# Beginning of the attention: whose engine makes the token sums, in which stages the first pair's queries and keys are made, and who orders TensorE

## The chip, the cores and the metric

The kernel runs on one core of a Trainium2 chip, as one launch. The metric is the device time in microseconds (us); lower is better. A core has a matrix engine (TensorE, PE in the profile; its weight loads are PEld), a vector engine (VectorE, DVE), a scalar engine (ScalarE, ACT), a general engine (GpSimd, POOL) and a queue that issues transfers (SyncE, SP). Each works through its own queue in order and waits for the others by semaphores.

## The reference

A block of three layers on x of 4 sequences by 256 tokens by 512 features, all in 32-bit floats:

```python
x = x + 0.5 * ffn(layernorm(x), A, B, Wr)      # 64 experts of rank 16, top 16 by softmax gates
x = x + attn(layernorm(x), wq, wkv, wo)
x = x + 0.5 * ffn(layernorm(x), A, B, Wr)

def attn(h, wq, wkv, wo):                      # 32 heads of 128
    q = (h @ wq) per head, first 128 of 192 columns
    k, v = (h @ wkv) per head
    scores = q @ k.T * 192 ** -0.5, causal
    return (softmax(scores) @ v) @ wo
```

The part that the change touches is the passage from the first feed-forward layer to the attention: the layer norm of the last tokens, and the queries, keys and values of the first heads.

## The kernel before

**Products in seven instead of eight.** Each large product is cut into 2x2 blocks, and sums of blocks let seven block products stand for eight. A product has a left side (tokens) and a right side (weights), and each needs its sums. `left_sums` (L166 to L175) makes the four sums of a left side, `right_sums` (L177) those of a right side. `seven` (L189) yields after each of the seven products M1, M2, M6, M5, M7, M3, M4; they use three PSUM banks: M1, M6, M7 and M4 one after the other in the first, M2 in the second, M5 and M3 in the third. After a product a reader takes the bank's sum out (L160, L139): ACT copies or VectorE adds. The next product into that bank waits for the reader.

Queries, keys and values use this scheme **twice**, one level inside the other. The tokens are held in `xop` as 7 outer by 7 inner operands, each 128x256. An outer index stands for one of the outer seven products (M1 0, M2 1, M7 2, M4 3, M5 4, M6 5, M3 6); the inner sums of one outer operand are the four sums of its own blocks (`inner_sums`, L450: inner 4, 5 and 6, and inner 2 overwritten in place). One **stage** makes one or two outer products with all their inner seven, and its readers add them to where they belong. So the values of a block of heads take stages for M1, M2, M6, M4 with M7, M5 and M3.

The weights are loaded block by block by SP and their sums made on GpSimd (`two_levels`, L505): first M5 and M6 (L525, L526), then the inner sums (L181, L184 to L186). M7 and M4 overwrite M1 and M2 in place once these have been used: `t3` (L518) and `t4` (L521), each 128x896.

**Loops.** Heads come in 16 pairs. `make_qk` (L594) makes queries and keys of a pair while the pair before attends, and `make_v` (L768) the values of two pairs at a time. The stages of pair 1 and later are M1 with M5, M2 with M6, M7 with M3, and M4. For the first pair they are M1, M2, M6 with M5, M7 with M3, and M4, in another set of readers. `qk` of a pair has four blocks of results; block 2 of the first pair is set to zero by a memset on GpSimd (L664), since M5's reader adds to it. In the stages that have an `into`, GpSimd adds two blocks of the result after the last read of each part (`done`, L650). Values have a form with M4 and M7 of their own (`m47`, L745): ACT copies one half of the bank, VectorE adds the other, and GpSimd sums the halves afterwards (L753).

**The beginning of the attention.** `norm_pair` (L457) is what the first layer calls after each pair of token tiles: normalise, transpose on TensorE, copy (L470 and L479 to L482) and form outer sums (L472 to L477). After the last tiles VectorE also forms outer 6's inner 2 and 3 (L484, L485). Then L896 to L915 interleave the first values' and the first pair's products, seven steps each at a time, with the last norm between the first and second seven, and inner sums between the third ones:

```python
    take(first_layer, 1)
    for _ in range(7):
        take(first_v, 1)
        take(first_qk, 1)
    inner_sums(5, 6, nc.vector)
    inner_sums(4, 5, nc.vector)
    inner_sums(2, 3, nc.gpsimd)
    inner_sums(6, 7, nc.gpsimd)
```

and `inner_sums(3, 4, nc.vector)` after the third seven. What is left of these streams goes into the eight units of pair 0's attention, by the letters in `FIRST_UNITS` (L942): g is the first values, f the first pair's queries and keys, v and q the next ones, b the second half of an attention block (`attend`, L867, after `probs`, L828).

**What sets the order.** A scheduling layer puts the instructions of each engine into an order of its own, by its estimate, unless an instruction is held with `keep_in_program_order`. Before, only the statistics of the norms (L103) and the first sum of the first output weights (L183) are held.

Of the kernel before, what the change touches and what calls it, by code (L numbers as in the profile page):

```python
# [32 lines left out]
def macaron_kernel(  # L33
# [11 lines left out]
    nc = tc.nc  # L45
# [117 lines left out]

    LAST = (3, 4, 5, 6)

    def left_sums(eng, s, a11, a12, a21, a22, *of):  # L166


        s3 = s[3] if len(s) > 3 else a21
        r11, r12, r21, r22 = of or (a11, a12, a21, a22)  # L170
        eng.tensor_tensor(s[0], r21, r22, ALU.add)  # L171
        eng.tensor_tensor(s[1], s[0], r11, ALU.subtract)
        eng.tensor_tensor(s[2], r12, s[1], ALU.subtract)
        eng.tensor_tensor(s3, r11, r21, ALU.subtract)
# [64 lines left out]
    def ffn(name, pairs, a_sums, b_sums, after, late):  # L239

        with ExitStack() as scope:
# [165 lines left out]
            for u in range(n + 1):  # L407
                hid = hidden(pairs[u], lefts[u], hgs) if u < n else iter(())
                tokens = prepare(pairs[u + 1]) if u + 1 < n else iter(())
                behind = after(work, pairs[u - 2]) if u > 1 else iter(())  # L410
                take(hid, 1)
                take(behind, 1)
                take(tokens, 1)
                take(hid, 2)
                take(tokens, 1)
                take(hid, 1)
                take(tokens, 1)
                if u < n:
# [12 lines left out]
        yield from after(None, pairs[n - 1])  # L431


# [13 lines left out]

    early = xop[:, 5:7, 6]

    def inner_sums(lo, hi, eng):  # L450
        o = slice(lo, hi)
        blocks = [xop[:, o, i] for i in range(4)]
        if lo == 0:
            blocks[2] = early
        left_sums(eng, [xop[:, o, i] for i in (4, 5, 6, 2)], *blocks)

    def norm_pair(work, pair):  # L457

        half, a = divmod(pair[0] // 2, 2)
        sl = slice(2 * a, 2 * a + 2)  # L460

        where = [xop[:, k, 4:6, :].rearrange("p a s -> p (a s)") for k in (5, 6)]
        tokens = normed(work, pair, "a", where)
        yield
        for i, xn in enumerate(tokens):
            cols = slice(i * P, (i + 1) * P)
            pt = turned_x(xn, f"a_{pair[i]}").rearrange("p (o c) k -> p o c k", o=2)
            a11, a12, s3, a22, s1, s2, _ = (xop[:, k, sl, cols] for k in range(7))
            if half:
                nc.scalar.copy(a22, pt[:, 1])  # L470
                if a:
                    nc.vector.tensor_tensor(s3[:, 0], early[:, 0, cols], pt[:, 0, 0], ALU.subtract)  # L472
                    nc.vector.tensor_tensor(s3[:, 1], a11[:, 1], pt[:, 0, 1], ALU.subtract)
                else:
                    nc.vector.tensor_tensor(s3, a11, pt[:, 0], ALU.subtract)
                nc.vector.tensor_tensor(s2, pt[:, 1], s3, ALU.subtract)
                nc.vector.tensor_tensor(s1, a22, pt[:, 0], ALU.add)  # L477
            elif a:
                nc.scalar.copy(early[:, :, cols], pt[:, :, 0])  # L479
                nc.scalar.copy(xop[:, 0:2, 3, cols], pt[:, :, 1])  # L480
            else:
                nc.scalar.copy(xop[:, 0:2, sl, cols], pt)  # L482
        if half and a:
            nc.vector.tensor_tensor(xop[:, 6, 2], early[:, 1], xop[:, 5, 2], ALU.subtract)  # L484
            nc.vector.tensor_tensor(xop[:, 6, 3], xop[:, 1, 3], xop[:, 5, 3], ALU.subtract)  # L485
        elif half:
            nc.vector.tensor_tensor(xop[:, 6, sl], xop[:, 1, sl], xop[:, 5, sl], ALU.subtract)
        elif a:
            inner_sums(0, 2, nc.vector)

    raw, rights, outs = {}, {}, {}

    def load_o(p):

# [10 lines left out]
    def two_levels(pool, bufs, name, blocks):  # L505

        t = {
            m: pool.tile([P, 7, P], F32, tag="w", name=f"{name}_{m}", bufs=bufs)  # L510
            for m in ("M1", "M5", "M2", "M3", "M6")
        }
        for m, k, n in (("M1", 0, 0), ("M5", 0, 1), ("M2", 1, 0), ("M3", 1, 1)):
            for i, view in enumerate(blocks(k, n)):
                nc.sync.dma_start(t[m][:, i : i + 3 : 2], view)

        def t3():
            nc.gpsimd.tensor_tensor(t["M1"], t["M6"], t["M1"], ALU.subtract)  # L518

        def t4():  # L520
            nc.gpsimd.tensor_tensor(t["M2"], t["M2"], t["M6"], ALU.subtract)  # L521

        def sums():
            plain = {m: v[:, 0:4] for m, v in t.items()}
            nc.gpsimd.tensor_tensor(plain["M5"], plain["M5"], plain["M1"], ALU.subtract)  # L525
# [12 lines left out]
    def load_qk(p):  # L538

        if p < NG:  # L540
            rights["qk", p] = two_levels(
                qkpool,
                6,
                f"wqk_{p}",
                lambda k, n: [
                    view[:, 2 * k : 2 * k + 2, p * HG + n, 0:DN] for view in (wq_v, wk_v)
                ],
            )()

    def load_v(k):  # L550

        if 2 * k < NG:
            raw["v", k] = two_levels(
                vpool,
                5,
                f"wv_{k}",
                lambda c, n: [
                    wv_v[:, 2 * c : 2 * c + 2, (2 * k + n) * HG + j] for j in range(HG)
                ],
            )  # L560

    with ExitStack() as scope:
# [31 lines left out]
    def make_qk(p):  # L594
# [33 lines left out]

            return read

        def branch(blocks, into=None):


            def read(r, ps):
                to = part(blocks, r)
                of = to if READS[r][2] else part(slice(1, 2), r).to_broadcast(to.shape)
                nc.vector.tensor_tensor(to, of, ps, ALU.add)  # L637
                done(r, into)

# [2 lines left out]
        def onto(blocks, into=None):  # L642
            def read(r, ps):
                to = part(blocks, r)
                nc.vector.tensor_tensor(to, to, ps, ALU.add)  # L645
                done(r, into)

            return read

        def done(r, into):  # L650

# [5 lines left out]
        if p > 0:  # L657
# [14 lines left out]
        yield from stage(("M4",), onto(slice(1, 2)), "d")  # L672
# [12 lines left out]
    def v_stages(k):  # L685
# [2 lines left out]
            return {}  # L688
        right, t3, t4 = raw["v", k]()
        u = 2 + 2 * (k % 2)  # L690

        def stage(ms, read, name, behind=None):
            def product(n, ps, first):
# [206 lines left out]
    for _ in range(7):  # L900
        take(first_v, 1)
        take(first_qk, 1)
    take(first_layer, 1)
    for _ in range(7):
        take(first_v, 1)
        take(first_qk, 1)
    inner_sums(5, 6, nc.vector)
    inner_sums(4, 5, nc.vector)
    inner_sums(2, 3, nc.gpsimd)
    inner_sums(6, 7, nc.gpsimd)  # L910
    for _ in range(7):
        take(first_v, 1)
        take(first_qk, 1)
    inner_sums(3, 4, nc.vector)
    take(first_qk, 7)  # L915

# [22 lines left out]
            "qoqobqoqo",  # L939
        ),  # L940
    )
    FIRST_UNITS = ("gfgfbgf", "gfgfbgfgf", "gvqvqbvqvq", "vqvqbvqvqvq", "vqvqbvqvqvq", "vqvqbvqq", "vqvqbqvqq", "vqvqbvqqq")  # L942
    LAST_UNITS = ("", "b", "oob", "oob", "oob", "oob", "ooob", "ooob")
    attending = []
    nothing = iter(())
    for p in range(NG):
# [92 lines left out]
```

## Time and profile before

| | us |
|---|---|
| median of 3 runs | 1184.9 (1184.69 to 1185.73) |
| the profiled execution | 1187.66 |
| its span | 1185.5 |
| chain that ended last: TensorE | 95% of the span |
| VectorE in it | 2% |
| transfers in it | 1% |
| VectorE sum of 128x512 (L824), mean | 0.688 |
| GpSimd sum of 128x256 (L654), mean | 0.728 |

The profile is of one execution, taken by the hardware profiler; its span is the stretch from the first to the last instruction. "Busy" counts the time in which an engine has an instruction in it, and an idle gap is put down to what released it, for example `<-DVE vbuf L721`. Columns of a timeline are start, length, engine, line, operation, output and inputs, partitions by elements, and how many like it follow each other. A 128x256 product is two records on TensorE. In the windows the clock is TensorE's granted one as a share of the full one.

### The profile page before, as it was taken

How to read it: one execution, taken by the hardware profiler on the slowest of the kernel's cores; microseconds unless marked ns; L12 is line 12 of the kernel's file. 1: busy time of each engine (PE TensorE's matmuls, PEld its weight loads, DVE VectorE, ACT ScalarE, POOL GpSimd, SP SyncE). 2: the span in 40 equal slices, each digit the busy share in tenths (PEclk: the TensorE clock that was granted, in tenths of full speed). 3: DMA queues.
4: the chain of work that ended last, by engine and by line, in shares of the span. 5: the costliest groups of instructions: out<-in, count | busy, mean ns of one | idle time of the engine just before them, and what ended most of it. 6: DMA issues, size and time to landing. Idle time of an engine off the chain costs nothing.

```text
span 1185.5 us, 18545 instructions
## 1 busy us (share of the span) xinstructions
PE 1166.3 (98%) x6492; PEld 1005.8 (85%) x6492; DVE 741.7 (63%) x1932; ACT 492.7 (42%) x1364; POOL 676.3 (57%) x933
## 2 busy tenths in 40 slices
PE   8999979999999999999999999999999999999998
PEld 5677869999999999999999898989898988875767
DVE  5444786566666666666576657665766666675432
ACT  4443314534443444344434443444443444546420
POOL 5611666986847684667575757657575644361110
PEclk9999989999999999999999999999999999999999
DMA  7001111111001101110111011110201000400001
GB/s 253 1 1 36 45 36 46 28 45 47 27 28 49 50 19 45 37 45 19 46 37 46 28 36 37 45 46 18 63 23 41 19 27 1 161 1 1 19 18 35
DMA packets 64940, 47.46 MB, mean 40 GB/s; under 512 B 4432, under 2 KB 55632, under 8 KB 64848
## 3 DMA queue, kind: packets, MB, share of 16 engines
q1 hardware_dynamic: 64848, 46.28, 13.2%
q8 instruction: 51, 0.84, 0.3%
q14 instruction: 41, 0.34, 0.1%
HBM read 44.17 MB, written 2.10 MB: 39 GB/s over the span
## 4 chain that ended last, share of the span: by engine, by line
PE 95%; DVE 2%; DMA 1%; ACT 1%; issue 0%; POOL 0%; SPq 0%; DVEq 0%; ACTq 0%
PE po L812 16%; PE pqk_c L607 8%; PE po_f L384 8%; PE pqk_a L607 8%; PE pqk_b L607 8%; PE ph_f L318 7%; PE pa L880 5%; PE ps L835 5%; PE pv_c L696 4%; PE pqk_d L607 4%; PE pv_b L696 4%; PE ptp L875 4%; PE ps L834 2%; PE pa L887 2%; PE pv_a L696 2%; PE pv_d L696 2%
## 5 line engine op out<-in xcount | busy, mean ns | idle before, releaser
L824 DVE TENSOR_TENSOR x<-x,po 128x512 f32<-128x512 f32 x224 | 153.9, 688 | 73.6 <-PE po L812 71.4
L854 ACT ACTIVATE s<-s,least 128x128 f32<-128x128 f32 (+1 forms) x256 | 114.5, 448 | 89.7 <-DVE least L843 89.7
L877 ACT COPY pT<-ptp 128x384 f32<-128x384 f32 x128 | 61.3, 479 | 207.6 <-PE ptp L875 207.6
L654 POOL TENSOR_TENSOR qk<-qk 128x256 f32<-128x256 f32 x128 | 92.7, 728 | 67.7 <-DVE qk L645 34.0
L864 ACT ACTIVATE s<-s,arden 128x128 f32<-128x128 f32 (+1 forms) x256 | 102.5, 448 | 51.5 <-DVE arden L862 51.2
L607 PE MATMUL pqk_a<-xop,wqk_M 128*128 128x256 f32 x448 | 116.9, 385 | 0.0
L607 PE MATMUL pqk_c<-xop,wqk_M 128*128 128x256 f32 x448 | 114.3, 381 | 0.0
L843 DVE CUSTOM_DVE_ANT_0 s<-ps,mask 128x128 f32<-128x128 f32 (+1 forms) x256 | 81.5, 356 | 51.0 <-PE ps L835 50.9
L345 POOL TENSOR_TENSOR hg_f<-hg_f,gate_f 128x512 f32<-128x512 f32 x32 | 33.6, 1057 | 132.1 <-DVE hg_f L331 68.9
L607 PE MATMUL pqk_b<-xop,wqk_M 128*128 128x256 f32 x420 | 106.9, 380 | 0.0
L645 DVE TENSOR_TENSOR qk<-qk,pqk_c 128x512 f32<-128x512 f32 x112 | 76.9, 688 | 43.0 <-PE pqk_c L607 33.8
L607 PEld LDWEIGHTS pqk_c<-xop,wqk_M 128*128 128x128 f32 x448 | 81.1, 191 | 9.7 <-DVE qk L645 1.0
L637 DVE TENSOR_TENSOR qk<-qk,pqk_b 128x512 f32<-128x512 f32 x105 | 72.2, 687 | 25.1 <-PE pqk_b L607 24.8
L181 POOL TENSOR_TENSOR wo<-wo 128x256 f32<-128x256 f32 x16 | 11.7, 728 | 128.0 <-DMA wo<-in_wo 112.6
L607 PEld LDWEIGHTS pqk_a<-xop,wqk_M 128*128 128x128 f32 x448 | 78.7, 194 | 6.5
L894 ACT COPY attn<-pa 128x256 f32<-128x256 f32 x128 | 47.5, 371 | 87.5 <-PE pa L887 87.5
L607 PEld LDWEIGHTS pqk_b<-xop,wqk_M 128*128 128x128 f32 x420 | 72.9, 191 | 6.1
L835 PE MATMUL ps<-qk 128*128 128x256 f32 x256 | 76.5, 381 | 0.0
L880 PE MATMUL pa<-pT,vbuf 128*128 128x256 f32 x256 | 76.2, 379 | 0.0
L812 PE MATMUL po<-wo,so 128*128 128x256 f32 x256 | 66.8, 383 | 1.7 <-DVE so L171 1.7
L812 PE MATMUL po<-to,attn 128*128 128x256 f32 x256 | 66.2, 381 | 0.9 <-DVE x L824 0.9
L607 PE MATMUL pqk_d<-xop,wqk_M 128*128 128x256 f32 x224 | 66.3, 380 | 0.0
(193 smaller groups left out, 2784.0 us busy)
## 6 DMA issues: line engine op xcount, KB each, us to landing
wv_M<-in_wkv SPq DMA_DIRECT2D x64, 128.0 KB, 2.5
wqk_M<-in_wq SPq DMA_DIRECT2D x64, 128.0 KB, 2.3
wqk_M<-in_wkv SPq DMA_DIRECT2D x64, 128.0 KB, 2.4
wo<-in_wo SPq DMA_DIRECT2D x16, 512.0 KB, 4.1
a_f<-in_a_t SPq DMA_DIRECT2D x8, 512.0 KB, 6.5
b_f<-in_b_t SPq DMA_DIRECT2D x4, 1024.0 KB, 8.8
x<-in_x SPq DMA_DIRECT2D x8, 256.0 KB, 8.2
out_x<-x SPq DMA_DIRECT2D x16, 128.0 KB, 1.7
```

The costliest lines, as they stand in the source:

```text
L318: nc.tensor.matmul(ps, lhsT=left[m][:, c, :], rhs=a_right[m][:, c, :], start=first and c == 0, stop=c == 1, skip_group_check=True,)
L384: nc.tensor.matmul(ps[:, 0:256], lhsT=left[m][:, c, :], rhs=b_right[m][:, c, :], start=first and c == 0, stop=c == 3, skip_group_check=True,)
L607: nc.tensor.matmul(ps[:, i * S : (i + 1) * S], lhsT=right[m][n], rhs=xop[:, OUTER[m], INNER[n]], start=first and i == 0, stop=True, skip_g ...
L654: nc.gpsimd.tensor_tensor(to, a, b, ALU.add)
L696: nc.tensor.matmul(ps[:, i * S + t * P : i * S + (t + 1) * P], lhsT=xop[:, OUTER[m], INNER[n], t * P : (t + 1) * P], rhs=right[m][n], star ...
L812: nc.tensor.matmul(ps[:, tt * 256 : (tt + 1) * 256], lhsT=outs[p][m][:, (2 * u + tt) * P : (2 * u + tt + 1) * P], rhs=right[m], start=firs ...
L824: nc.vector.tensor_tensor(to, to, ps.rearrange("p (t d) -> p t d", t=2), ALU.add)
L835: nc.tensor.matmul(ps[:, P : 3 * P], lhsT=qT[:, P : 2 * P], rhs=kT, start=True, stop=True)
L843: nc.vector.tensor_tensor_reduce(out=s[:, cols], in0=ps[:, cols], in1=mask_f[:, cols], scale=-SCALE, scalar=-TAKEN, op0=ALU.add, op1=ALU.m ...
L854: nc.scalar.activation(s[:, cols], s[:, cols], AF.Exp, bias=least[:, i : i + 1], scale=-1.0, accum_out=den[:, i : i + 1],)
L864: nc.scalar.mul(s[:, cols], s[:, cols], rden[:, i : i + 1])
L880: nc.tensor.matmul(po[:, 0 : 2 * P], lhsT=v_of(p, j, 2 * b), rhs=pT[:, 0 : 2 * P], start=True, stop=False,)
```

## The change

- `left_sums` can hold its sums in program order and call something ahead of its last sum. `inner_sums` holds those of outer 2 and above.
- The inner sums of outer 5, 4 and 3, and the two sums for outer 6 (`last_outer`), move from VectorE to GpSimd; all are held, in this order: the values' `t3`, the queries' and keys' `t3`, outer 5 with `last_outer` ahead of its last sum, the values' `t4`, outer 2, outer 3, the queries' and keys' `t4`, outer 4, outer 6.
- The first pair's queries and keys are made in the values' stages: M1, M2, M6, M4 with M7 (with a reader `m47` like the values'), M5, M3. The base for M2 is block 3, and the memset goes.
- Values and queries with keys alternate for seven steps through the first three stages. The last norm begins after two of the first seven; its second part, with the transposes, comes after all seven (for that, a `yield` more in `ffn`).
- From there to the end of pair 0's attention TensorE's instructions stand in program order (`manual_schedule`), with new `FIRST_UNITS`. The weights of pair 1 are loaded after the first pair's M5.
- The first sum M5 of the weights of queries and keys for pair 1 and of the values for the second block is held in program order.

```diff
-    def left_sums(eng, s, a11, a12, a21, a22, *of):
+    def left_sums(eng, s, a11, a12, a21, a22, *of, pinned=False, between=None):
...
+            if to is s3 and between is not None:
+                between()
+            made = eng.tensor_tensor(to, a, b, op)
+            if pinned:
+                tc.keep_in_program_order(made)
...
+        yield
         yield from after(None, pairs[n - 1])
...
-        left_sums(eng, [xop[:, o, i] for i in (4, 5, 6, 2)], *blocks)
+        left_sums(eng, [xop[:, o, i] for i in (4, 5, 6, 2)], *blocks, pinned=lo > 0, between=between)
+
+    def last_outer():
+
+        for of, i in ((early[:, 1], 2), (xop[:, 1, 3], 3)):
+            tc.keep_in_program_order(
+                nc.gpsimd.tensor_tensor(xop[:, 6, i], of, xop[:, 5, i], ALU.subtract)
+            )
...
-        if half and a:
-            nc.vector.tensor_tensor(xop[:, 6, 2], early[:, 1], xop[:, 5, 2], ALU.subtract)
-            nc.vector.tensor_tensor(xop[:, 6, 3], xop[:, 1, 3], xop[:, 5, 3], ALU.subtract)
...
+        def m47(r, ps):
+
+            both, one, two, base = (part(slice(*k), r) for k in ((1, 3), (1, 2), (2, 3), (3, 4)))
+            if READS[r][2]:
+                nc.vector.tensor_tensor(both, both, ps, ALU.add)
+            else:
+                nc.scalar.copy(one, ps[:, 0:1])
+                nc.vector.tensor_tensor(two, base, ps[:, 1:2], ALU.add)
+            if r in LAST:
+                nc.gpsimd.tensor_tensor(one, one, two, ALU.add)
...
-            nc.gpsimd.memset(dst[:, 2], 0.0)
-            yield from stage(("M1",), fresh(slice(1, 2)), "m")
-            t3()
-            yield from stage(("M2",), branch(slice(0, 1)), "n")
-            t4()
-            yield from stage(("M6", "M5"), onto(slice(1, 3), 3), "a")
+            turns["qk"] = t3, t4
+
+            yield from stage(("M1",), fresh(slice(3, 4)), "m")
+            yield from stage(("M2",), branch(slice(0, 1), of=slice(3, 4)), "n")
+            yield from stage(("M6",), onto(slice(3, 4)), "o")
+            yield from stage(("M4", "M7"), m47, "r")
+            yield from stage(("M5",), onto(slice(2, 4)), "s")
+            load_qk(p + 1)
+            yield from stage(("M3",), onto(slice(3, 4)), "u")
+            return
...
+    written_out = ExitStack()
+    written_out.enter_context(tc.manual_schedule(engines={mybir.EngineType.PE}))
...
+    first_products(2)
     take(first_layer, 1)
...
+    first_products(5)
+    take(first_layer, 1)
+
+    tc.keep_in_program_order(turns["v"][0]())
+    tc.keep_in_program_order(turns["qk"][0]())
+    first_products(7)
+    inner_sums(5, 6, nc.gpsimd, last_outer)
+    tc.keep_in_program_order(turns["v"][1]())
     inner_sums(2, 3, nc.gpsimd)
+    inner_sums(3, 4, nc.gpsimd)
+    tc.keep_in_program_order(turns["qk"][1]())
+    inner_sums(4, 5, nc.gpsimd)
     inner_sums(6, 7, nc.gpsimd)
...
+    first_products(7)
...
+        "gggg",
+        "gggfffbfffffvfvfvfv",
+        "fvfvfvbfvfvfvf",
+        "fvfvbfvfv",
+        "qqvqbqqvq",
+        "qqvqbqqvq",
+        "qqvqbqqvq",
+        "qqvqbqqvq",
...
+        written_out.close()
         sums_o(p)
```

More of the change, by code (lines that the diff above doesn't have):

```diff
@@ L164, in macaron_kernel @@
     LAST = (3, 4, 5, 6)
-    def left_sums(eng, s, a11, a12, a21, a22, *of):
+    def left_sums(eng, s, a11, a12, a21, a22, *of, pinned=False, between=None):
         s3 = s[3] if len(s) > 3 else a21
         r11, r12, r21, r22 = of or (a11, a12, a21, a22)
[L171 to L174, printed above, removed]
+        for to, a, b, op in (
+            (s[0], r21, r22, ALU.add),
+            (s[1], s[0], r11, ALU.subtract),
+            (s[2], r12, s[1], ALU.subtract),
+            (s3, r11, r21, ALU.subtract),
+        ):
+            if to is s3 and between is not None:
[3 more added lines that the diff above has]
+                tc.keep_in_program_order(made)
         return {"M1": a11, "M2": a12, "M3": s[2], "M4": a22, "M5": s[0], "M6": s[1], "M7": s3}
@@ L448, in macaron_kernel, with inner_sums @@
     early = xop[:, 5:7, 6]
-    def inner_sums(lo, hi, eng):
+    def inner_sums(lo, hi, eng, between=None):
         o = slice(lo, hi)
@@ L482, in norm_pair @@
                 nc.scalar.copy(xop[:, 0:2, sl, cols], pt)
-        if half and a:
-            nc.vector.tensor_tensor(xop[:, 6, 2], early[:, 1], xop[:, 5, 2], ALU.subtract)
-            nc.vector.tensor_tensor(xop[:, 6, 3], xop[:, 1, 3], xop[:, 5, 3], ALU.subtract)
-        elif half:
+        if half and not a:
             nc.vector.tensor_tensor(xop[:, 6, sl], xop[:, 1, sl], xop[:, 5, sl], ALU.subtract)
-        elif a:
+        elif a and not half:
             inner_sums(0, 2, nc.vector)
-    raw, rights, outs = {}, {}, {}
+    raw, rights, outs, turns = {}, {}, {}, {}
     def load_o(p):
@@ L503, in sums_o, with two_levels @@
         rights["o", p] = right_sums(nc.gpsimd, [t[:, i, :] for i in range(3)], *b, pinned=p == 0)
-    def two_levels(pool, bufs, name, blocks):
+    def two_levels(pool, bufs, name, blocks, pinned):
         t = {
@@ L517, in t3 @@
         def t3():
-            nc.gpsimd.tensor_tensor(t["M1"], t["M6"], t["M1"], ALU.subtract)
+            return nc.gpsimd.tensor_tensor(t["M1"], t["M6"], t["M1"], ALU.subtract)
         def t4():
-            nc.gpsimd.tensor_tensor(t["M2"], t["M2"], t["M6"], ALU.subtract)
+            return nc.gpsimd.tensor_tensor(t["M2"], t["M2"], t["M6"], ALU.subtract)
         def sums():
             plain = {m: v[:, 0:4] for m, v in t.items()}
-            nc.gpsimd.tensor_tensor(plain["M5"], plain["M5"], plain["M1"], ALU.subtract)
+            first = nc.gpsimd.tensor_tensor(plain["M5"], plain["M5"], plain["M1"], ALU.subtract)
+            if pinned:
+                tc.keep_in_program_order(first)
             nc.gpsimd.tensor_tensor(plain["M6"], plain["M3"], plain["M5"], ALU.subtract)
@@ L547, in load_qk @@
                 ],
+                p == 1,
             )()
@@ L559, in load_v @@
                 ],
+                k == 1,
             )
@@ L629, in fresh, with branch @@
             return read
-        def branch(blocks, into=None):
+        def branch(blocks, into=None, of=slice(1, 2)):
+            base = of
             def read(r, ps):
                 to = part(blocks, r)
-                of = to if READS[r][2] else part(slice(1, 2), r).to_broadcast(to.shape)
+                of = to if READS[r][2] else part(base, r).to_broadcast(to.shape)
                 nc.vector.tensor_tensor(to, of, ps, ALU.add)
@@ L644, in read @@
                 to = part(blocks, r)
-                nc.vector.tensor_tensor(to, to, ps, ALU.add)
+                of = ps if ps.shape == to.shape else ps.to_broadcast(to.shape)
+                nc.vector.tensor_tensor(to, to, of, ALU.add)
                 done(r, into)
             return read
+        def m47(r, ps):
[7 more added lines that the diff above has]
+                nc.gpsimd.tensor_tensor(one, one, two, ALU.add)
         def done(r, into):
@@ L690, in v_stages @@
         u = 2 + 2 * (k % 2)
+        if k == 0:
+            turns["v"] = t3, t4
+            t3 = t4 = None
         def stage(ms, read, name, behind=None):
@@ L897, in macaron_kernel, with first_products @@
     load_qk(0)
+    written_out = ExitStack()
+    written_out.enter_context(tc.manual_schedule(engines={mybir.EngineType.PE}))
     first_qk = make_qk(0)
     first_v = chain(*(v_by[0][m] for m in ("M1", "M2", "M6", "M4M7")))
-    for _ in range(7):
-        take(first_v, 1)
-        take(first_qk, 1)
-    take(first_layer, 1)
[L904 to L908, printed above, removed]
+    def first_products(n):
+        for _ in range(n):
+            take(first_v, 1)
+            take(first_qk, 1)
+    first_products(2)
+    take(first_layer, 1)
+    first_products(5)
[5 more added lines that the diff above has]
+    tc.keep_in_program_order(turns["v"][1]())
     inner_sums(2, 3, nc.gpsimd)
+    inner_sums(3, 4, nc.gpsimd)
+    tc.keep_in_program_order(turns["qk"][1]())
+    inner_sums(4, 5, nc.gpsimd)
     inner_sums(6, 7, nc.gpsimd)
[L911 to L915, printed above, removed]
+    first_products(7)
     UNITS = (
@@ L941, in macaron_kernel @@
     )
-    FIRST_UNITS = ("gfgfbgf", "gfgfbgfgf", "gvqvqbvqvq", "vqvqbvqvqvq", "vqvqbvqvqvq", "vqvqbvqq", "vqvqbqvqq", "vqvqbvqqq")
+    FIRST_UNITS = (
+        "gggg",
[6 more added lines that the diff above has]
+        "qqvqbqqvq",
+    )
     LAST_UNITS = ("", "b", "oob", "oob", "oob", "oob", "ooob", "ooob")
```

## The prediction

> **What bounds the kernel now.** I read the page's busy shares, then the row of slices, then the waits of TensorE where the slices dip, then its timeline around each wait.
>
> ```profile
> PE 1166.3 (98%) x6492; PEld 1005.8 (85%) x6492; DVE 741.7 (63%) x1932; ACT 492.7 (42%) x1364; POOL 676.3 (57%) x933
> PE   8999979999999999999999999999999999999998
> ```
>
> TensorE is busy 98% and the bound almost everywhere. The only dip between the ends is the sixth digit, 119 to 178 us (29.6 us a slice): the end of the first feed-forward layer and the start of the attention, which is what the change rewrites. From 300 to 1180 us TensorE is busy 877.2 of 880, so nothing is to be had later. Its waits from 128 to 166 us, and that stretch in pieces of 5 us:
>
> ```profile
> PE pv_o L696 <- DVE vbuf L721: 6.1, 1, 6.1
> PE pv_n L696 <- DVE vbuf L721: 1.4, 1, 1.4
> PE pv_a L696 <- ACT vbuf L727: 0.9, 2, 0.5
> ...
> 140.00:145.00 5.00, 3.60 (x26) 3.26 (x26) 4.87 (x13) 0.71 (x1) 4.84 (x7) 1.00 0.00 0
> 145.00:150.00 5.00, 5.00 (x34) 4.64 (x33) 4.74 (x9) 0.00 (x0) 4.92 (x8) 1.00 0.00 0
> 150.00:155.00 5.00, 0.54 (x3) 0.13 (x2) 5.00 (x4) 0.00 (x0) 5.00 (x4) 1.00 0.00 0
> 155.00:160.00 5.00, 3.36 (x10) 2.92 (x11) 3.84 (x9) 0.00 (x0) 1.02 (x2) 0.52 0.00 0
> 160.00:165.00 5.00, 5.00 (x25) 4.50 (x25) 3.69 (x8) 0.00 (x0) 0.73 (x1) 0.80 0.00 0
> ```
>
> The columns are length, busy PE, PEld, DVE, ACT, POOL, then TensorE's granted clock. Three waits are 8.4 us; and behind the longest the clock is 0.52 and 0.80. The price of that is in TensorE's own timeline, with VectorE and GpSimd beside it:
>
> ```profile
> 149.94 0.60 PE L835 MATMUL ps<-qk 128*128 128x256 f32 x2
> 156.64 1.22 PE L696 MATMUL pv_o<-wv_M,xop 128*128 128x128 f32 x4 [6.10 <-DVE vbuf L721]
> 157.65 3.62 PE L607 MATMUL pqk_a<-xop,wqk_M 128*128 128x256 f32 x8
> 161.06 1.06 PE L696 MATMUL pv_o<-wv_M,xop 128*128 128x128 f32 x4
> ...
> 150.84 2.25 POOL L521 TENSOR_TENSOR wv_M<-wv_M,wv_M 128x896 f32<-128x896 f32 x1
> 151.08 2.29 DVE L173 TENSOR_TENSOR xop<-xop 128x256 f32<-128x256 f32 x1
> 153.05 2.24 POOL L521 TENSOR_TENSOR wqk_M<-wqk_M,wqk_M 128x896 f32<-128x896 f32 x1
> 153.29 2.29 DVE L172 TENSOR_TENSOR xop<-xop 128x256 f32<-128x256 f32 x1
> 155.50 0.41 DVE L174 TENSOR_TENSOR xop<-xop 128x256 f32<-128x256 f32 x1
> ```
>
> At full clock a record of 256 columns starts every 0.216 us and one of 128 every 0.110. So I count what is lost as start to next start minus records times these. After the last score product (149.94 + 0.43) nothing starts for 6.27. Then the eight pqk_a records take 3.41 to the next start instead of 1.73: lost 1.68; with the rows around them 0.57 + 1.68 + 0.42 + 0.25 = 2.92 for the slow clock. The first-stage products pv_a lose 0.63 + 0.73 + 0.19, the pv_n stop 1.56 + 0.11, small ones 0.27. **12.7 us in all** from 130.28 to 174 us; from there to 262 us nothing more is lost.
>
> **The change part by part.**
>
> *TensorE's amount of work* is the same: the first pair's seven products by seven are 49 before (7+7+14+14+7) and after (7+7+7+14+7+7), 0.43 us each. Up to the end of the layer (130.28 us) its order is the same too. So the gain is 12.7 minus what the new order loses.
>
> *Token sums.* Fourteen sums of 128x256 (three times L171 to L174, and L484, L485) leave VectorE. There they took 13.6 us (0.97 each); on GpSimd the eight beside them start every 0.69 us from 144 to 148. Here a rule speaks against the change: the Trainium skill, GPSIMD Engine Reference, "4.1 Engine selection", sends elementwise work to VectorE and calls GpSimd about 2x slower with two inputs. By the rule with the trace's undisturbed times (0.41 here, 0.72 there) the move costs 14 x 0.31 = 4.3 us; by the rows it saves, as a sum that meets GpSimd's 2.25 us one takes 2.29. SBUF - State Buffer, "SBUF: two separate sides", has the reason: a VectorE operation with two SBUF inputs and a GpSimd one exclude each other for a whole instruction. VectorE's remaining reads have one input in PSUM, and beside a GpSimd busy 4.84 of 5 us they start every 0.35 (142.1 to 147.4). So I take the rows. The 6.27 stop goes: VectorE's queue no longer holds sums ahead of the reads.
>
> *GpSimd's queue, in order, and its due times.* The memset (0.96) goes; the first values' L518 waits for TensorE's last first-stage product (136.0): two L518 136.2 to 140.4 (2.1 each), one wo sum 0.7 (its transfer landed by 133.5), then outer 5's sums and L484, L485: s1 done 142.5, all six 145.3; L521 for the values 147.4; outer 2 150.2; outer 3 152.9 (the part that is due first 151.6); L521 for queries and keys 155.0; outer 4 157.8; outer 6 160.6. Due at TensorE: 146.5, 151.5, 153.3, 158.7, 166.6. The tightest cover is 1.7 us.
>
> *TensorE's order by hand,* with these terms: values product 0.44, query/key product 0.43, pair 0.87 (M4 and M7 together 0.87 for either); reader starts 0.20 after a product, TensorE 0.06 after the reader; VectorE 0.33 for 128x256, 0.60 for 128x512, ACT copy 0.37.
> - First stage (M1), 130.3 to 136.4: values and keys alternate, a bank is wanted back 1.74 after its product and the round trip is 1.07 (130.28 to 131.35), so the pv_a waits go. The statistics stand behind two reads in VectorE's queue and begin 132.6, not 130.8; with 4.2 from there to the second normalised tile (as at 130.82 to 135.02) it is ready 136.9, its transposes wanted 136.8: lost 0.1.
> - Second stage (M2), to 144.7: its first reads stand behind six xop operations that wait for the transposes' copies: values' M6 wants 139.1 and gets 139.8, keys' 140.2 and 140.8. Lost 1.3 (before 1.67).
> - Third (M6), to 150.9: two reads a pair are 0.67 of 0.87. Nothing lost.
> - Values' M4 with M7: the copies stand behind two exponentials on ACT (0.4 + 0.19 + 0.51 + 0.18): M6 wants 153.3, gets 154.1. Lost 0.8; keys' M4 with M7, behind the next softmax, 0.2. It runs 159.5 to 166.4.
> - M5 of both: VectorE needs 2 x 0.60 = 1.20 a pair and TensorE 0.87; over seven pairs and a softmax (0.85) 9.3 against 7.7 with 1.0 of lag allowed. Lost 1.2. Keys' reads here also wait for GpSimd's sums of M4 and M7, which stand behind four sums of the next values' M2, whose transfer waits for the values' stage at 159.5 (four issues of 0.47, 2.5 to land: 163.9). Due 169.9, done 167.5. The second head quarter's scores wait for the last, 168.4, due 170.2.
> - M3 of both: lost 0.2. Pair 1's keys in "qqvqb" order: ACT's copies stand behind exponentials, 0.5; its last stage 0.2.
>
> Sum 0.1 + 1.3 + 0.8 + 0.2 + 1.2 + 0.2 + 0.7 = 4.5. No stop exceeds 0.8 us, and the 1.40 one before left the clock at 1.00, so the 2.92 stays away. **Gain 12.7 - 4.5 = 8.2 us.** The unknown is the hand-written order, of which the trace has nothing: below, 0 lost where neighbours fill in (gain 12.7); above, every interleaved pair at VectorE's 1.20 (first rival but one). I take 4.5, nearest to the rows.
>
> *Next pair's loads* are issued after M5 instead of after M7 with M3. Their sums end on GpSimd at about 182, wanted 184.5 onward: hidden by 2.5. But GpSimd is full from 216 to 243:
>
> ```profile
> 239.26 2.09 POOL L521 TENSOR_TENSOR wv_M<-wv_M,wv_M 128x896 f32<-128x896 f32 x1
> ...
> 242.38 1.06 PE L696 MATMUL pv_c<-wv_M,xop 128*128 128x128 f32 x8
> ```
>
> This sum ends 241.3 for a product at 242.4: 1.1 of cover. TensorE comes here 8.2 earlier, 234.2; my queue brings the sum to 232.7. Cover 1.5, so nothing is lost, but it is the next thing to be late.
>
> The profiled execution took 1187.66 (span 1185.5), the median is 1184.9. I carry the 8.2 over: 1179.5 for a profiled one, **1176.7 as median**.
>
> **Rivals.**
> - *GpSimd's queue is late (0.20).* Sums that met VectorE's took 0.90 instead of 0.69 (149 to 151 us). If all do, twelve sums before outer 3's are 2.5 late: 0.8 beyond cover; the M5 reads 4 late: 2; the 242 point 1 to 2. Gain 8.2 - 3.8 = 4.4: 1180.5. Against it: hardly a VectorE operation with two SBUF inputs is left there.
> - *The waits overlap more than my sum (0.12).* A read counted late may run ahead, as each engine's queue follows: only the second stage and M5 lose, 2: gain 10.7, 1174.2.
> - *The fixed order makes TensorE wait for readers (0.06, slower).* The place is the five alternating stages, 35 pairs. If VectorE needs 1.20 a pair in all of them instead of in one, 35 x 0.33 = 11.6, with 2.3 from M4/M7 and softmax and 1.5 from late sums 15.4: loss 2.7, 1187.6. It decides from 12.7, a read pair of 1.16; the rows show 0.67 to 0.70 for three of the stages.
> - *It does not take effect (0.03):* the sums' wait of 6.27 stays because GpSimd reaches s1 of outer 5 not at 142.5 but past 150; then about 1184.
>
> **Numbers.** Likeliest 0.59 at 1176.7, own range 1174.5 to 1179. With the first two rivals 1173.8 to 1181 holds 8 of 10. No change can be told within 0.2% (2.4 us). Faster 0.91, same 0.03, slower 0.06.
>
> **What would show it.** Right: no TensorE wait over 1 us between 130 and 185, PEclk 1.00 there, VectorE without L171 to L174 on xop after 130, GpSimd's L521 ending near 147 and 155, TensorE's first product of pair 1's second unit about 8 us earlier. Wrong: TensorE waiting for POOL xop, wv or qk sums; a stop long enough for PEclk to fall; or losses in M5 beyond 2 us.

## The result, and the profile after

The changed kernel took **1177.56 us** (median of 4 runs, 1176.83 to 1178.34), the kernel before on the same chip 1184.8 (4 runs, 1184.33 to 1185.73): a ratio of 0.9937, with a 95% interval of 0.9924 to 0.9949. Run again later it took 1176.71 (5 runs, 1176.28 to 1177.13) against 1185.31, a ratio of 0.9923 (0.9911 to 0.9936). The forecast was 1176.7.

The profiled execution after took 1176.98 us with a span of 1175.2, that is 10.3 less span than before. Not all of this is the change's. The first product of the attention (pv_a) starts at 130.28 us before and at 128.15 after, although of what stands ahead of it only a memset on GpSimd (0.96 us at 117.8 us) was taken away; the last section shows that these 2.13 us are there long before it. From that product to the end of the span it is 1185.5 - 130.28 = 1055.22 us before and 1175.2 - 128.15 = 1047.05 after: **8.17 less**. I use this stretch, "from pv_a to the end", for all profiles below, since it leaves the uneven beginning out.

The page's busy time and slices of the changed kernel, to be laid beside those of before:

```profile
PE 1164.4 (99%) x6492; PEld 1003.0 (85%) x6492; DVE 732.3 (62%) x1925; ACT 493.9 (42%) x1368; POOL 681.4 (58%) x942
PE   9999999999999999999999999999999999999998
```

The dip in the sixth digit is gone. TensorE's waits from 128 to 185 us, and its windows (length, busy PE, PEld, DVE, ACT, POOL, granted clock, DMA share, GB/s):

```profile
PE pv_c L732 <- DVE vbuf L757: 0.4, 1, 0.4
PE pqk_s L624 <- DVE qk L664: 0.4, 1, 0.4
PE pqk_n L624 <- DVE qk L655: 0.4, 1, 0.4
PE pv_n L732 <- DVE vbuf L757: 0.3, 1, 0.3
```

```profile
140.00:145.00 5.00, 5.00 (x36) 4.72 (x35) 4.79 (x13) 0.00 (x0) 4.92 (x6) 1.00 0.00 0
145.00:150.00 5.00, 5.00 (x36) 4.71 (x35) 4.61 (x13) 0.08 (x1) 4.69 (x8) 1.00 0.06 15
150.00:155.00 5.00, 4.57 (x39) 4.36 (x39) 2.54 (x8) 3.12 (x10) 4.84 (x6) 1.00 0.12 33
155.00:160.00 5.00, 4.95 (x33) 4.26 (x33) 2.96 (x10) 2.53 (x8) 4.84 (x7) 1.00 0.54 139
160.00:165.00 5.00, 4.95 (x25) 4.04 (x23) 2.69 (x5) 1.13 (x4) 4.84 (x10) 1.00 0.10 29
```

Where TensorE had 0.54 and 3.36 of 5 us, it now has 4.57 and 4.95, at a clock of 1.00. The price is in the POOL column: GpSimd has no free room from 140 to 165 us. Its queue, with three marks of TensorE's below it, in the timeline of the same kernel:

```profile
138.95 2.33 POOL L180 TENSOR_TENSOR xop<-xop 128x256 f32<-128x256 f32 x3
141.24 1.42 POOL L470 TENSOR_TENSOR xop<-xop 128x256 f32<-128x256 f32 x2
142.62 0.73 POOL L180 TENSOR_TENSOR xop<-xop 128x256 f32<-128x256 f32 x1
143.30 2.09 POOL L534 TENSOR_TENSOR wv_M<-wv_M,wv_M 128x896 f32<-128x896 f32 x1
145.35 6.00 POOL L180 TENSOR_TENSOR xop<-xop 128x256 f32<-128x256 f32 x8
151.30 2.09 POOL L534 TENSOR_TENSOR wqk_M<-wqk_M,wqk_M 128x896 f32<-128x896 f32 x1
153.35 6.02 POOL L180 TENSOR_TENSOR xop<-xop 128x256 f32<-128x256 f32 x8
...
142.59 0.61 PE L732 MATMUL pv_o<-wv_M,xop 128*128 128x128 f32 x4
149.39 1.95 PE L732 MATMUL pv_c<-wv_M,xop 128*128 128x128 f32 x16
164.78 0.59 PE L624 MATMUL pqk_s<-xop,wqk_M 128*128 128x256 f32 x2
```

The 22 token sums stand in the order in which the products want them, some 0.75 us apart on the mean: 0.80 where a sum needs the one just ahead of it (the three of the first row), 0.69 where it does not (the two of L470). To compare with the prediction's times, which stand on the clock of the profile before, add 2.13.

### The profile page after: what moved, and what is told of

Same layout as the page of the kernel before. It is cut to its first block, busy times and chain, and to the rows that moved or that the text cites. A ratio compares the mean times of both kernels' runs of the same rounds, so it can differ in the third digit from the quotient of the medians.

```text
span 1175.2 us, 18548 instructions
## 1 busy us (share of the span) xinstructions
PE 1164.4 (99%) x6492; PEld 1003.0 (85%) x6492; DVE 732.3 (62%) x1925; ACT 493.9 (42%) x1368; POOL 681.4 (58%) x942
## 4 chain that ended last, share of the span: by engine, by line
PE 95%; DMA 1%; DVE 1%; ACT 1%; issue 0%; SPq 0%; DVEq 0%; ACTq 0%
PE po L848 16%; PE po_f L392 8%; PE pqk_a L624 8%; PE pqk_c L624 8%; PE pqk_b L624 8%; PE ph_f L326 7%; PE ps L871 5%; PE pa L916 5%; PE pv_c L732 4%; PE pqk_d L624 4%; PE pv_b L732 4%; PE ptp L911 4%; PE ps L870 2%; PE pa L923 2%; PE pv_e L732 2%; PE pv_d L732 2%
## 5 line engine op out<-in xcount | busy, mean ns | idle before, releaser
L684 POOL TENSOR_TENSOR qk<-qk 128x256 f32<-128x256 f32 x120 | 87.1, 728 | 57.4 <-DVE qk L655 27.9
L624 PE MATMUL pqk_a<-xop,wqk_M 128*128 128x256 f32 x420 | 107.9, 380 | 0.0
L624 PE MATMUL pqk_c<-xop,wqk_M 128*128 128x256 f32 x420 | 107.1, 380 | 0.0
L664 DVE TENSOR_TENSOR qk<-qk,pqk_c 128x512 f32<-128x512 f32 x105 | 72.3, 688 | 40.8 <-PE pqk_c L624 32.5
L624 PEld LDWEIGHTS pqk_c<-xop,wqk_M 128*128 128x128 f32 x420 | 76.1, 190 | 8.6 <-DVE qk L664 0.3
L624 PEld LDWEIGHTS pqk_a<-xop,wqk_M 128*128 128x128 f32 x420 | 72.5, 191 | 6.2 <-POOL wqk_M L192 0.3
L848 PE MATMUL po<-wo,attn 128*128 128x256 f32 x256 | 64.7, 379 | 0.0
```

Of the source, the lines that this page charges most:

```text
L624: nc.tensor.matmul(ps[:, i * S : (i + 1) * S], lhsT=right[m][n], rhs=xop[:, OUTER[m], INNER[n]], start=first and i == 0, stop=True, skip_g ...
L684: nc.gpsimd.tensor_tensor(to, a, b, ALU.add)
L848: nc.tensor.matmul(ps[:, tt * 256 : (tt + 1) * 256], lhsT=outs[p][m][:, (2 * u + tt) * P : (2 * u + tt + 1) * P], rhs=right[m], start=firs ...
```

## The experiments

**Either half of the change alone.** Two kernels part the change: one has the sums on GpSimd and the old stages and order, the other the new stages and order and the sums on VectorE. The first, against the kernel before (`left_sums`, `inner_sums` and `last_outer` as changed):

```diff
-    inner_sums(5, 6, nc.vector)
-    inner_sums(4, 5, nc.vector)
+    inner_sums(5, 6, nc.gpsimd, last_outer)
+    inner_sums(4, 5, nc.gpsimd)
     inner_sums(2, 3, nc.gpsimd)
     inner_sums(6, 7, nc.gpsimd)
+    inner_sums(3, 4, nc.gpsimd)
...
-    inner_sums(3, 4, nc.vector)
```

> The kernel before, with one part of the change alone: the sums of outer blocks 5, 4 and 3 and outer block 6's last two sums go to GpSimd, pinned in the order 5, 4, 2, 6, 3. Stages and TensorE's order stay the scheduler's. Theory (the lock between VectorE's sums and GpSimd's is the main loss): the stop of 6.27 us and the slow clock of 2.92 us behind it go, but the third stage still multiplies M5 beside M6, so outer block 4's sums, which end some 3 us behind outer block 5's, make a stop of about 3 us at 145 to 149 us: a gain of 4 to 6 us, 1179 to 1181 us, TensorE waiting there for GpSimd and not for VectorE. Rival (the stages and the written order bring the gain): at most 2 us, 1183 to 1185 us.

It took 1186.85 us (20 runs) against 1185.26, a ratio of 1.0013 (1.0006 to 1.0020): **no gain at all, a loss of 1.6**. Both theories had a gain, and mine fell. The stop of about 3 us came (1.6, for GpSimd's sum), but behind it stands a larger one. TensorE's longest wait of that kernel, and its timeline there:

```profile
PE pqk_c L619 <- DVE qk L657: 8.0, 1, 8.0
```

```profile
146.54 10.36 POOL L180 TENSOR_TENSOR xop<-xop 128x256 f32<-128x256 f32 x14
156.86 2.07 POOL L533 TENSOR_TENSOR wv_M<-wv_M,wv_M 128x896 f32<-128x896 f32 x1
158.89 0.72 POOL L180 TENSOR_TENSOR xop<-xop 128x256 f32<-128x256 f32 x1
159.57 2.07 POOL L533 TENSOR_TENSOR wqk_M<-wqk_M,wqk_M 128x896 f32<-128x896 f32 x1
161.59 1.41 POOL L180 TENSOR_TENSOR xop<-xop 128x256 f32<-128x256 f32 x2
162.96 2.77 POOL L666 TENSOR_TENSOR qk<-qk 128x256 f32<-128x256 f32 x4
...
163.72 1.48 DVE L657 TENSOR_TENSOR qk<-qk,pqk_c 128x512 f32<-128x512 f32 x2 [8.25 <-POOL qk L666]
164.46 6.39 PE L619 MATMUL pqk_c<-xop,wqk_M 128*128 128x256 f32 x20 [7.99 <-DVE qk L657]
```

In the old stages GpSimd adds two blocks of the queries and keys after M6 with M5 (here L666, the `done` of the reader), and VectorE's reads of the next stage (M7 with M3) need these sums. VectorE wanted the first at 155.5 us; GpSimd was in its row of token sums until 162.96. So the stop of 6.27 behind VectorE's sums was exchanged for one of 8.0 behind GpSimd's queue, followed by a clock of 0.60 (160 to 165 us) and 0.72 (165 to 170 us). This holds for the one order of GpSimd's sums that was run; an order with L666 ahead of the token sums that are needed later was not tried.

The second, against the changed kernel:

```diff
-                nc.gpsimd.tensor_tensor(xop[:, 6, i], of, xop[:, 5, i], ALU.subtract)
+                nc.vector.tensor_tensor(xop[:, 6, i], of, xop[:, 5, i], ALU.subtract)
...
-    inner_sums(5, 6, nc.gpsimd, last_outer)
+    inner_sums(5, 6, nc.vector, last_outer)
...
-    inner_sums(3, 4, nc.gpsimd)
+    inner_sums(3, 4, nc.vector)
...
-    inner_sums(4, 5, nc.gpsimd)
+    inner_sums(4, 5, nc.vector)
```

> The changed kernel with the sums of outer blocks 5, 3 and 4 and the last two of block 6 back on VectorE (14 sums), stages and written order as changed. Theory (the exclusive lock): the VectorE sums that fall beside GpSimd's sums take some 2.3 us each in place of 0.41, the readers of the third stage's products queue behind them, and TensorE stops: 6 to 9 us slower than the changed kernel, 1183 to 1187 us, the granted clock below 1.00 behind the stop. Rival (only VectorE's room counts: 14 x 0.41 = 5.7 us, which VectorE has free for the most part): under 3 us slower, 1178 to 1180 us.

It took 1187.55 us (15 runs), a ratio of 1.0023 to before (1.0015 to 1.0031): **some 10 us slower than the changed kernel**, more than expected. Its timeline shows the lock (the exclusion of which the prediction speaks) operation by operation:

```profile
141.97 2.09 POOL L534 TENSOR_TENSOR wv_M<-wv_M,wv_M 128x896 f32<-128x896 f32 x1 [3.40 <-PE pv_n L732]
144.01 3.50 POOL L180 TENSOR_TENSOR xop<-xop 128x256 f32<-128x256 f32 x4
147.47 2.25 POOL L534 TENSOR_TENSOR wqk_M<-wqk_M,wqk_M 128x896 f32<-128x896 f32 x1
...
142.70 1.64 DVE L180 TENSOR_TENSOR xop<-xop 128x256 f32<-128x256 f32 x1
144.26 0.41 DVE L757 TENSOR_TENSOR vbuf<-vbuf,pv_o 128x256 f32<-128x256 f32 x1
144.59 0.61 DVE L180 TENSOR_TENSOR xop<-xop 128x256 f32<-128x256 f32 x1
147.72 3.15 DVE L180 TENSOR_TENSOR xop<-xop 128x256 f32<-128x256 f32 x2
150.79 0.41 DVE L757 TENSOR_TENSOR vbuf<-vbuf,pv_o 128x256 f32<-128x256 f32 x1
154.72 0.74 DVE L180 TENSOR_TENSOR xop<-xop 128x256 f32<-128x256 f32 x2
...
151.25 0.70 PE L624 MATMUL pqk_o<-xop,wqk_M 128*128 128x256 f32 x2 [4.41 <-DVE vbuf L757]
154.18 1.22 PE L732 MATMUL pv_o<-wv_M,xop 128*128 128x128 f32 x4 [2.23 <-DVE vbuf L757]
```

VectorE's sum that begins inside GpSimd's 2.09 ends 0.28 us behind it. Beside GpSimd's shorter sums it takes 0.61 to 0.94, and these 0.88 each in place of 0.73. Taken one by one in the trace, all ten VectorE sums here that meet a GpSimd sum end 0.28 us behind the end of that sum, whether it is a long or a short one, and so do, at 0.28 to 0.29, the nine of the kernel before that meet one between 130 and 160 us. So how long a sum takes depends on when it begins. Once GpSimd is idle (from 153.2) two of them take 0.74 together. A read with one input in PSUM (L757) takes 0.41 all the time. So it is the meeting of two-input SBUF operations that costs, not VectorE's load; and the reads that stand behind the sums stop TensorE, as before. One thing differs from the kernel before: here the sums are held in program order on VectorE too. How much of the 10 us this order makes was not tried.

**The written order.** One line of the changed kernel taken away:

```diff
-    written_out.enter_context(tc.manual_schedule(engines={mybir.EngineType.PE}))
```

> The changed kernel with TensorE's written order taken away, so that the scheduler orders its instructions; sums and stages as changed. Theory: the order is worth little, because the sums on GpSimd are pinned and come in time either way: 1176.5 to 1179.5 us, no stop over 2 us on TensorE between 128 and 165 us. Rival (the written order carries a large part): 1181 us or more, with stops where a product is put ahead of its sum.

1176.96 us (4 runs), 0.9930 (0.9916 to 0.9945): as the changed kernel, and from pv_a to the end 1047.14 in place of 1047.05. TensorE's longest wait from 126 to 190 us is 0.5. By the count of the prediction the scheduler loses 3.8 us between 128 and 182 us, and the written order also 3.8, in other places: the scheduler 1.5 in the first stage, the written order 1.0 in the M5 stage. The third part of the change is worth nothing as a whole. The four kernels, by their ratio to before, are: sums alone 1.0013, stages and order alone 1.0023, sums and stages 0.9930, all three 0.9937.

**How late GpSimd may be.** In the changed kernel's `left_sums`, eight more sums ahead of all the others:

```diff
-            made = eng.tensor_tensor(to, a, b, op)
+            for _ in range(9 if to is s[0] and between is not None else 1):
+                made = eng.tensor_tensor(to, a, b, op)
...
```

> The changed kernel with outer block 5's first sum made nine times and not once: 8 more GpSimd sums of 0.75 us each, some 6.0 us of delay for all sums behind it. It measures how late GpSimd may be. Theory (cover of 4.0 us at outer block 5 and 1.7 us at outer block 3, one delay not added to the other): 4 to 5 us slower than the changed kernel, TensorE waiting for GpSimd first in the third stage and then in the values' M4 and M7 stage. Rival (GpSimd has room, its sums are needed only later): under 1 us slower.

1182.06 us (8 runs), 4.5 slower than the 1177.56 of the changed kernel, and from pv_a to the end 1051.40 in place of 1047.05: as the theory had it. Counted from pv_a, the last sum of outer block 5 ended 6.45 us later. TensorE lost 2.64 at the third stage's third product (waiting for GpSimd, 2.48 of it), 1.68 more in that stage, and 0.87 in the values' M4 and M7 stage. The 1.68 are slow records, which neither theory had: the window behind the first stop shows a clock of 0.66.

```profile
145.00:150.00 5.00, 3.47 (x13) 3.17 (x14) 1.27 (x3) 0.00 (x0) 4.84 (x7) 0.66 0.00 0
```

They need not have made this kernel slower: at full clock TensorE would have come 1.68 earlier to the sums of outer block 3 and, as GpSimd sets their time, waited that much longer. So the cover at outer block 5 is 6.45 - 2.64 = 3.8 us, and at outer block 3 6.45 - 2.64 - 1.68 - 0.87 = 1.3. GpSimd is in time in the changed kernel, but not by much.

**The slow clock by itself.** In a3_sums_back, the kernel with the sums on VectorE, TensorE's stops are filled with products of zeros into a bank that nobody reads. The first attempt was too large:

```diff
-    first_products(7)
+    fill = ps_s.tile([P, 512], F32, tag="s", name="fill")
+
+    def busy(n):
+        for _ in range(n):
+            nc.tensor.matmul(fill[:, 0:P], lhsT=zeros, rhs=zeros, start=True, stop=True)
+
+    first_products(2)
+    busy(8)
+    first_products(1)
+    take(first_v, 1)
+    busy(36)
+    take(first_qk, 1)
+    busy(16)
+    first_products(3)
```

> The kernel of a3_sums_back (14 sums on VectorE) with 60 added 128x128 products of zeros, 0.11 us each, into a PSUM tile that nobody reads, in the places where its TensorE stood still (8 ahead of the third stage's third product, 36 in the stop of 4.4 us, 16 in the one of 2.2 us). They add work and leave nothing out. Theory (the slow clock behind a long stop is a cost of its own, put at 2.92 us for the kernel before): the stops stay, the granted clock stays at 1.00 from 150 to 160 us, and the run is 1.8 to 2.9 us faster than a3_sums_back, about 1185 us. Rival (the records behind the stop only look long, the time is the wait's): as a3_sums_back, 1187 to 1188 us.

1190.36 us, 2.8 slower than a3_sums_back. A product of zeros is two records, 0.22 us and not 0.11: 60 of them are 13.9 us (1.95 + 8.20 + 3.73), more than the stops. This run says nothing of the clock's price, so it was made again with 5, 20 and 11.

> As a5_filled_stop, with fewer products of zeros: 5, 20 and 11. In a5_filled_stop one of them took 0.22 us and not 0.11 (72 records of 0.11 us for 36 products), so that they filled 13.9 us where the three stops of a3_sums_back had 1.3, 4.6 and 2.5 us. Here they fill 1.1, 4.4 and 2.4 us. Theory (the slow clock is a cost of its own): granted clock 1.00 throughout, 1.8 to 2.6 us faster than a3_sums_back, 1185 to 1186 us. Rival (the slow clock's records cost nothing): as a3_sums_back, 1187 to 1188 us.

The windows of a3_sums_back and then of a6_filled_to_size, 150 to 160 us:

```profile
150.00:155.00 5.00, 1.52 (x6) 1.12 (x7) 5.00 (x12) 0.00 (x0) 3.03 (x4) 0.70 0.00 0
155.00:160.00 5.00, 5.00 (x22) 4.40 (x22) 3.48 (x11) 0.00 (x0) 0.00 (x0) 0.62 0.00 1
```

```profile
150.00:155.00 5.00, 4.95 (x41) 4.58 (x40) 5.00 (x11) 0.00 (x0) 2.99 (x4) 1.00 0.00 0
155.00:160.00 5.00, 4.76 (x33) 4.20 (x34) 4.02 (x15) 1.13 (x5) 0.00 (x0) 1.00 0.25 65
```

The clock stays at 1.00, so it does follow how busy TensorE is. But the gain lies between the two theories: 1186.91 us (20 runs, 1.0011 to 1.0024 of before) against 1187.55 (1.0015 to 1.0031), 0.6 us on two chips, which these intervals hardly part. In the traces, from pv_a to pair 1's first product it is 63.60 us in place of 65.00, and to the end 1056.84 in place of 1057.68. By the prediction's count a3_sums_back loses 2.13 us in slow records behind its stop. At full clock the same products lose 0.86 of it to reads that VectorE, busy 5.00 of 5 us there, has not yet made. By these two kernels and c2_delay8, slow records are a loss only as far as nothing else would have held these products.

**What is left, and a faster kernel.** Between 128 and 182 us the changed kernel still loses 3.8 us. Three moves in the changed kernel's written order went for it together:

```diff
-            yield from stage(("M5",), onto(slice(2, 4)), "s")
-            load_qk(p + 1)
             yield from stage(("M3",), onto(slice(3, 4)), "u")
+            yield from stage(("M5",), onto(slice(2, 4)), "s")
+            load_qk(p + 1)
...
-    first_products(5)
+    first_products(7)
     take(first_layer, 1)
...
-    first_products(7)
+    first_products(5)
...
     first_products(7)
+    take(first_v, 1)
...
-        "gggg",
+        "ggg",
```

> The changed kernel with three further moves in the written order: the first pair's M3 stage ahead of its M5 stage, so that VectorE has 0.93 us of readers in a pair of products and not 1.20; the last transposes two pairs of products later; one values' M4 and M7 product ahead of the first scores. Theory (what is lost after the change, some 4.2 us, is readers that come late by their turn): about 2 us faster than the changed kernel, 1175 to 1176 us. Rival (the waits only move to the next product): 1177 to 1178 us.

1185.75 us (12 runs), 8 slower than the changed kernel. TensorE waits 6.5 us at pair 1's first stage, for the weights' sums on GpSimd. Its queue in the timeline:

```profile
172.04 0.46 POOL L194 TENSOR_TENSOR wqk_M<-wqk_M 128x128 f32<-128x128 f32 x1
181.02 1.27 POOL L541 TENSOR_TENSOR wv_M<-wv_M,wv_M 128x512 f32<-128x512 f32 x1 [8.52 <-PE pv_e L732]
...
187.56 1.26 POOL L538 TENSOR_TENSOR wqk_M<-wqk_M,wqk_M 128x512 f32<-128x512 f32 x1
```

The loading had moved with the M5 stage, and with it the sums of pair 1's weights (L538) came behind a sum for the next values (L541), which by the profile is released by TensorE's last product of the values (pv_e): 8.5 us in which GpSimd stands. The move itself was sound: the M5 and M3 stages lost nothing, where the changed kernel loses 1.0. The other two were not: the second stage lost 1.1 with the later transposes (1.2 in the changed kernel), and the value product ahead of the scores left a wait of 0.8 for a softmax in place of one of 0.4. With the loading ahead of both stages, again against the changed kernel:

```diff
+            load_qk(p + 1)
+            yield from stage(("M3",), onto(slice(3, 4)), "u")
             yield from stage(("M5",), onto(slice(2, 4)), "s")
-            load_qk(p + 1)
-            yield from stage(("M3",), onto(slice(3, 4)), "u")
```

> The changed kernel with the first pair's M3 stage ahead of its M5 stage, as in b4_all, but with the loading of pair 1's weights for queries and keys put ahead of both, so that on GpSimd's queue they stay ahead of the values' weights. Theory (b4_all lost 6.7 us only because pair 1's weights came behind a GpSimd sum that waited for the values' last product; the readers' turn was right): the 1.0 us lost in the M5 stage goes, and the first product of pair 1 does not wait: 0.6 to 1.1 us faster than the changed kernel, about 1176.6 us. Rival (the weights' buffers come free only behind M5's last product, wherever the loading is written): 4 us or more slower than the changed kernel, TensorE waiting for GpSimd at some 182 to 200 us.

1176.51 us (4 runs), 0.9923 (0.9908 to 0.9938). From pv_a to pair 1's first product 53.20 us in place of 54.22, and no wait for GpSimd: the theory's 1.0. The other way was to leave what lies behind the third stage to the scheduler:

```diff
     inner_sums(6, 7, nc.gpsimd)
     first_products(7)
+    written_out.close()
```

> The changed kernel with TensorE's written order ended behind the third stage, the scheduler ordering the rest of the first pair. Theory (the written order keeps the first two stages free of waits, 1.2 us lost there against 2.9 us where the scheduler orders them, and loses 2.3 us behind them where the scheduler loses some 1.0): the better half of each, 1 to 1.5 us faster than the changed kernel, about 1176.3 us. Rival (what is lost behind the third stage is GpSimd's or VectorE's pace, not the order): as the changed kernel, 1177 to 1178 us.

1176.30 us (4 runs), 0.9921 (0.9906 to 0.9936); in the trace 52.89 us in place of 54.22. As these differences are about as large as the spread of one kernel's runs, the changed kernel, this one, and both moves together were run once more beside each other.

> The changed kernel itself, for a comparison with d2_scheduler_late and b7_both on one chip: 1177 to 1178 us.

> The kernel of b6_scheduler_late with more rounds. In its trace the first product of pair 1 came 52.89 us behind the first of the attention, in the changed kernel's 54.22. Theory (this 1.3 us is kept to the end): 1.1 to 1.5 us faster than d1_changed. Rival (it is given back later, or was the chip's): within 0.6 us of d1_changed.

> The moves of b5_m3_first_load and b6_scheduler_late together. Theory (both take away the same loss, readers that come late in the M5 stage): as d2_scheduler_late within 0.5 us. Rival (two losses, which add): 2 to 2.4 us faster than d1_changed.

| | median us (runs) | from pv_a to the end |
|---|---|---|
| before | 1185.31 (25) | 1055.22 |
| d1_changed | 1176.71 (5) | 1046.99 |
| d2_scheduler_late | 1175.16 (4) | 1045.34 |
| b7_both | 1175.19 (4) | 1045.31 |

The runs of d2_scheduler_late (1174.91 to 1175.59) lie below all runs of d1_changed (1176.28 to 1177.13): **1.55 us faster, a version that beats both kernels**, at 0.991 (0.9895 to 0.9925) of before. The medians alone are a weak witness, since this same kernel had 1176.30 as b6_scheduler_late; the stretch from pv_a to the end is not, with 1045.40 and 1045.34 in its two profiles and 1047.05 and 1046.99 in the changed kernel's two. The 1.65 gained there is what pair 1's first product had gained (54.22 - 52.89 = 1.33) and a little more. The two moves do not add; both take the same loss away.

## Why the prediction was right, point by point

- **The sum.** 8.2 was forecast, 8.17 measured from pv_a to the end of the profiles, and 7.24 and 8.6 by the two comparisons of medians. That the first two agree to a few hundredths is luck: single terms were off by 0.4 one way and 0.25 the other (below), and by the same count of records the changed kernel loses 8.6 less in the first 132 us from pv_a and 0.4 more, in small pieces, in all that follows, where the prediction had nothing.
- **What the change removes.** The 6.27 stop and the slow clock behind it, the pv_a waits and the long pv_n stop are gone. That the stop was the lock's is shown by a3_sums_back, where stops of the same kind come back (1.2, 4.4 and 2.2 us). That all of the 2.92 was the slow clock's own is not: in that kernel, with 2.13 counted in the same way, only 0.8 (to the end) to 1.4 (to pair 1) came back when the clock was held up. For this change it made no difference, since stop and slow clock went together.
- **The rule against the row.** The rule would have had the move to GpSimd cost 4.3 us. The rows were right: with the stages of the change, 14 sums on GpSimd in place of VectorE make the kernel 10 us faster.
- **GpSimd's times.** On the clock of before, outer 5's sums were forecast to end at 145.3, and ended at 145.48 (143.35 + 2.13); the values' L521, now L534, at 147.4 and 147.52; the one for queries and keys at 155.0 and 155.52; outer 6 at 160.6 and 161.50. They are up to 0.9 late, as a sum took 0.75 and not 0.69: the forecast's row of starts had five sums of which none needed the one just ahead of it. The covers of 4.0 and 1.7 us were 3.8 and 1.3. At the later point, forecast with a cover of 1.5, the sum ends at 230.1 and its product starts at 231.67: 1.6.
- **The losses, step by step.** First stage 0.1 forecast, 0.06 measured; second 1.3 and 1.17; third 0 and 0; values' M4 with M7 0.8 and 0.90; keys' M4 with M7 **0.2 and 0.63**; M5 1.2 and 1.04; M3 0.2 and 0; pair 1's keys and last stage 0.7 and about 0.45. That makes 4.5 and 4.2. The mis-sized term is the keys' M4 with M7: two losses of 0.31, at the stage's third product (159.38 us) and at its sixth (162.95). The list of waits doesn't have them, but the timelines do. Ahead of the first:

```profile
158.50 0.37 ACT L675 COPY qk<-pqk_r 128x256 f32<-128x256 f32 x1 [0.49 <-PE pqk_r L624]
158.91 0.42 DVE L676 TENSOR_TENSOR qk<-qk,pqk_r 128x256 f32<-128x256 f32 x1 [0.44 <-ACT qk L675]
159.38 0.92 PE L624 MATMUL pqk_r<-xop,wqk_M 128*128 128x256 f32 x3
```

The reader `m47` takes the bank out in two halves, and VectorE's half begins only when ACT's copy is done. The bank is free 1.08 after its product gave way to the next (158.30); that one product fills 0.86 of it, which leaves 0.22, and the next record takes 0.10 more; the sixth product (ACT 162.07, VectorE 162.47) is the same again. So the loss is not a softmax's, as the forecast had it, but the two halves one after the other. In b6_scheduler_late, where products of the values or of the attention stand between most of these, the two losses aren't there.
- **What the prediction gave no part to.** It took the written order as a source of risk, with the trace having nothing on it. As a whole it neither helps nor hurts (a2_no_hand_order); its part behind the third stage costs 1.55 (d2_scheduler_late). And it took the sums and the stages as two items of one sum. They are not: each alone, in the form that was run, is worth less than nothing. That the new stages make GpSimd's own results (L678) due only at the first M5 read, 165.7 us, and not at the end of the third stage, as L666 was, gives GpSimd the time for the token sums; this reading rests on the wait for L666 in a1_sums_alone. The due times of the change were worked out with this in them, so the total came out right without the reason having been named.
- **The rivals.** GpSimd late: no wait for GpSimd appears, though its sums were slower than forecast. Waits that overlap more: no, 4.2 of 4.5 were lost. TensorE waiting for readers everywhere: its place was the five alternating stages, of which only M5, with two reads of 0.60, needs 1.20 a pair; in the third stage TensorE loses nothing. No effect: no.

## What to carry to other kernels

When work is moved to an engine with free time, ask what that engine has to deliver next and when: here the same 14 sums cost 1.6 us or saved 10, by the due time of the sums behind them. When a stage is moved in the program, its loads move too, and with them their place in every queue; a loading whose sums came behind a wait of 8.5 us on GpSimd undid a sound move. And a long sum on one engine is to be laid beside every two-input operation in SBUF on the other before its mean time is believed.

## What the hardware showed beside this

The start of the first layer is not the same in each execution, whatever the kernel. The windows from 20 to 25 us of the profiles before and after, each with TensorE's rows there:

```profile
20.00:25.00 5.00, 3.25 (x8) 1.69 (x9) 0.10 (x2) 2.37 (x5) 5.00 (x5) 0.71 0.89 241
21.75 0.84 PE L364 MATMUL pth_f<-ident,hg_f 128*128 128x128 f32 x4 [2.54 <-POOL hg_f L345]
22.39 3.43 PE L318 MATMUL ph_f<-at_f,fxs_f 128*128 128x512 f32 x4
```

```profile
20.00:25.00 5.00, 3.95 (x17) 2.18 (x18) 1.66 (x5) 3.19 (x7) 5.00 (x4) 1.00 0.84 223
20.96 0.66 PE L372 MATMUL pth_f<-ident,hg_f 128*128 128x128 f32 x4 [1.69 <-POOL hg_f L353]
21.45 1.88 PE L326 MATMUL ph_f<-at_f,fxs_f 128*128 128x512 f32 x4
```

TensorE waits for an operation of GpSimd (hg_f) that ends 0.78 us later in the first, and the four records behind the longer stop take 3.43 in place of 1.88, at a clock of 0.71. From 28.6 us to pv_a the two profiles keep a distance of 2.12 to 2.13 us, so all of it arises here: pv_a starts at 130.28 us before and at 128.15 after. In b6_scheduler_late (clock 0.66) it starts at 129.90, in b5_m3_first_load (0.75) at 129.57. That is some 2 us of span without any change in the code of this layer, about what separates the runs of one kernel. Why GpSimd comes later in one execution than in another is open. For small changes it means: count from a mark behind it.

How long a stop must be to lower the clock can't be given as one figure. At this place stops of 2.16 (b5_m3_first_load), 2.20 (b6_scheduler_late) and 2.54 us (before) were followed by a lower clock, one of 2.35 (a1_sums_alone) and those up to 2.04 (a5_filled_stop) were not; later, one of 2.48 in c2_delay8 was.
